# Self attention of a decoder layer: when the scores are made and when their exponentials are issued

## The chip, the cores and the metric

The kernel runs on one core of a Trainium2 chip. The time is device microseconds (us) of one execution; before the change it is 2971.65 us, the median of three runs (2970.52 to 2972.86). The core has one matrix engine (PE, with its weight loads shown apart as PEld), the engines DVE, ACT and POOL, and SP, which issues the DMAs. Matrix results land in PSUM, which this kernel uses as eight banks of 512 fp32 columns on 128 partitions.

## The reference, cut to what matters

A small encoder over 2 x 77 rows gives the memory; then a decoder layer runs over x, which is (2, 2048, 512) in fp32: causal self attention, cross attention, and a feed-forward of width 2048. There are 16 heads of 32 columns. The part that the change touches is the causal self attention:

```
y = y + _mha(yn, yn, ..., sb)                 # yn = _ln(y), sb = relative bias + causal mask
# in _mha, for each of the 16 heads:
scores = einsum('bhqd,bhkd->bhqk', q, k) / sqrt(32) + bias[None]
attn = softmax(scores, axis=-1)
out = einsum('bhqk,bhkd->bhqd', attn, v)
```

## The kernel before

**Units, pieces, visits.** A unit is one tile of 128 query rows (`t`) of one block of 512 rows (`m`, 0 to 3), for one group of four heads (`g`), in one batch entry (`b`). Unit `n` runs over `b`, `m`, `g`, `t` in this order: 128 units, numbered 0 to 127, with sixteen in a block. A unit at row tile `i = 4m + t` needs the `i + 1` key tiles up to its own; `pieces` cuts them into runs of at most four tiles. In block 3 the runs are 4, 4, 3, 2, or 4, 4, 4 and 2, 3 or 4; in block 2 there are three, in block 1 two, in block 0 one.

**Five steps.** I call them S, E, T, V and the slot. S (`scores`, lines 344 to 393) makes one piece of scores for four heads: eight matmuls (line 361) into four banks, one bank for each head; DVE then copies each bank to SBUF and takes its row maximum (line 370), adding the bias for the last two tiles (line 377). When the unit's last piece is there, line 384 reduces the pieces' maxima to one negated maximum, once for each head, right behind that head's last copy. E is the exponential of one head's whole row, in place, on ACT (line 387). T (`turn`, 397 to 418) transposes the probabilities of up to two pieces: in blocks 1 to 3 each load takes one key tile of all four heads into one bank (line 411), and the bank is copied to `pts`, three of eight loads by DVE (line 415) and then five by ACT (line 417). V (`values`, 420 to 440) multiplies by the values into one bank (line 428), and ACT copies that bank out (line 436, or 439 for pieces after the first). The slot (`slot(n + 1)`) issues other work: a projection (lines 206, 217, 230 and 242, eight matmuls of 512 columns), transposes for the softmax's division (line 453) and for the norm (line 294), in some blocks parts of the encoder or of the first cross attention, and all DMA issues, on SP.

**The order is written out by hand.** Every engine runs its instructions in the order in which the program issues them. `bank()` deals the eight banks in turn: an S takes four, a T one for each load, a V one, a projection one. The loop from line 1264 makes a visit for each pair of pieces:

```
turn(pair)                       # T, then one E: exps(1) at line 418
if ends and n + 1 < end:
    slot(n + 1)
if may_score():
    score_next()
while may_score() and (len(pair) > 1 or units[n][1] == 0):
    score_next()
exps(3 if units[n][1] == 1 else 1)
values(pair)                     # V
```

A unit of block 2 or 3 has two visits, called a and b below ("visit 36b"); the slot is in b. `may_score` (line 1246) lets a piece of unit `n` be scored once unit `n - 2` has been transposed that far, because the two share a place in `pp`. E of blocks 1 to 3 waits in the list `late_exps` until `exps(k)` issues the first `k` of it; in block 0 it is issued at once. Ahead of a unit's first T, everything of that unit that still stands in `late_exps` is issued.

**Two orders, written out.** S38(0-3) is the score step of key tiles 0 to 3 of unit 38, E38.0 the exponential of its head 0, T8 a transposition of eight key tiles. Block 2 and block 3 before:

```
36a: T7 E37.0 S38(0-3) E37.1 V7
36b: T2 E37.2 slot S38(4-7) E37.3 V2
37a: T8 S38(8-10) S39(0-3) S39(4-7) E38.0 V8
37b: T2 E38.1 slot S39(8-11) E38.2 V2
38a: E38.3 T8 E39.0 S40(0-3) S40(4-6) E39.1 V8
...
52a: T8 E53.0 S54(0-3) S54(4-7) E53.1 V8
52b: T5 E53.2 slot S54(8-11) S54(12-14) E53.3 V5
53a: T8 E54.0 ...
```

Of the kernel before, what the change touches and what calls it, by code (L numbers as in the profile page):

```python
# [11 lines left out]
AF = mybir.ActivationFunctionType  # L12
ALU = mybir.AluOpType
AX = mybir.AxisListType
# [3 lines left out]
P = 128  # L18
# [4 lines left out]
HC = P // HD  # L23
# [31 lines left out]
def tile_encoder_decoder(ctx: ExitStack, tc: tile.TileContext, ins, out):  # L55
    nc = tc.nc
# [92 lines left out]
    with (  # L149
# [20 lines left out]
        def bank():  # L170

            i = count["bank"] % count["banks"]
            count["bank"] += 1
            return psum[:, i, :]
# [6 lines left out]
        def rows4(r):  # L181
            return slice(r * HD, (r + 1) * HD)


        nTs, qTs, ots, sums_of = {}, {}, {}, {}
# [132 lines left out]
        units = [(b, m, g, t) for b in range(B) for m in range(NMB) for g in range(NC) for t in range(TB)]  # L318
# [13 lines left out]
        def probabilities(n):  # L332
            w = (units[n][1] + 1) * MB
            at = END - HC * w if n % 2 else 0
            return [pp[:, at + r * w : at + (r + 1) * w] for r in range(HC)]

        late_exps = []

        def exps(k):

            for _ in range(min(k, len(late_exps))):
                late_exps.pop(0)[1]()

        def scores(n, k0, kn):
            b, m, g, t = units[n]
            i = m * TB + t
            if k0 == 0:
                state[n] = {
                    "p": probabilities(n),
                    "mx": sm.tile([P, HC, 8], F32, name="mx", tag="mx"),  # L350
                    "nm": sm.tile([P, HC], F32, name="nm", tag="nm"),
                    "col": 0,
                }
                if t == 0:
                    sums_of[b, m, g] = sm.tile([P, TB, HC], F32, name="sums", tag="sums")
            st = state[n]
            last = k0 + kn == i + 1
            q = qTs[b, m, g]
            banks = [bank() for _ in range(HC)]
            for r in range(HC):  # L360
                nc.tensor.matmul(  # L361
                    banks[r][:, : kn * P], q[rows4(r), ts(t, P)], kT[rows4(r), g, k0 * P : (k0 + kn) * P],
                    start=True, stop=True,
                )
            far = max(0, kn - 2) if last else kn
            col = st["col"]
            for r in range(HC):
                p, s, c = st["p"][r], banks[r], col
                if far:
                    nc.vector.tensor_scalar(  # L370
                        p[:, k0 * P : (k0 + far) * P], s[:, : far * P], 1.0, None, ALU.mult, ALU.max,
                        accum_out=st["mx"][:, r, c : c + 1],
                    )
                    c += 1
                if last:
                    w = (kn - far) * P
                    nc.vector.tensor_tensor_reduce(  # L377
                        p[:, (i + 1) * P - w : (i + 1) * P], s[:, far * P : kn * P],
                        biases[b, m, g][:, r, 2 * P - w :], 1.0, LOWEST, ALU.add, ALU.max,
                        accum_out=st["mx"][:, r, c : c + 1],  # L380
                    )
                    c += 1
                    nm = st["nm"][:, r : r + 1]
                    nc.vector.tensor_reduce(nm, st["mx"][:, r, :c], AX.X, ALU.max, negate=True)  # L384

                    def run(p=p[:, : (i + 1) * P], nm=nm, to=sums_of[b, m, g][:, t, r : r + 1]):
                        nc.scalar.activation(p, p, AF.Exp, bias=nm, accum_out=to)  # L387

                    if m:
                        late_exps.append((n, run))  # L390
                    else:
                        run()
            st["col"] = c

        got = {}

        def turn(pieces):

            first = units[pieces[0][0]][1] == 0
            loads = []  # L400
            for n, k0, kn in pieces:
                ks = range(k0, k0 + kn)
                if first:
                    loads += [[(n, k, r) for k in ks] for r in range(HC)]
                else:
                    loads += [[(n, k, r) for r in range(HC)] for k in ks]
            for o, load in enumerate(loads):
                pt = bank()
                pts = in_turn("pts", pts_all).rearrange("p (x q) -> p x q", q=P)
                for x, (n, k, r) in enumerate(load):  # L410
                    nc.tensor.transpose(pt[:, ts(x, P)], state[n]["p"][r][:, ts(k, P)], ident)  # L411
                    got[n, k, r] = pts[:, x, :]
                w = len(load) * P
                if o % 2 if first else o < 3 * len(loads) // 8:
                    nc.vector.tensor_copy(pts[:, : len(load), :], pt[:, :w])  # L415
                else:
                    nc.scalar.copy(pts[:, : len(load), :], pt[:, :w])  # L417
            exps(1)

        def values(pieces):  # L420

            n = pieces[0][0]
            b, m, g, t = units[n]
            ks = [k for _, k0, kn in pieces for k in range(k0, k0 + kn)]
            ot = bank()[:, :P]
            for k in ks:
                for r in range(HC):
                    nc.tensor.matmul(  # L428
                        ot[rows4(r), :], vv[:, k, ts(g * HC + r, HD)], got.pop((n, k, r)),
                        start=(k == ks[0]), stop=(k == ks[-1]),  # L430
                    )
            if t == 0 and ks[0] == 0:
                ots[b, m, g] = in_turn("oT", oT_all)
            dst = ots[b, m, g][:, ts(t, P)]
            if ks[0] == 0:
                nc.scalar.copy(dst, ot)
            else:
                more = sm.tile([P, P], F32, name="more", tag="more", bufs=1)
                nc.scalar.copy(more, ot)  # L439
                nc.gpsimd.tensor_tensor(dst, dst, more, ALU.add)  # L440
# [538 lines left out]
        def slot(n):  # L979
            for f in light[n]:  # L980
                f()
            for _, run, _ in jobs[n]:
                load_next()
                run(loaded[ran[0]])
                ran[0] += 1
            if n == 5:
                load_next()
# [35 lines left out]
        def w_1_load(i):  # L1023

            nc.sync.dma_start(w_1[:, :, ts(i, D)], wchunk("dec_ff1_wT", i * D))
# [220 lines left out]
        def may_score():  # L1246

            if at[0] == len(stream):
                return False
            n, k0, kn = stream[at[0]]  # L1250
            same = n >= 2 and units[n][:2] == units[n - 2][:2]
            return n < 2 or turned_to[n - 2] >= (min(k0 + kn, size[n - 2]) if same else size[n - 2])

        def score_next():
            n, k0, kn = stream[at[0]]
            scores(n, k0, kn)
            scored_to[n] = k0 + kn
            at[0] += 1
# [4 lines left out]
        i = 0  # L1263
        while i < len(stream):
            n = stream[i][0]
            pair = [p for p in stream[i : i + 2] if p[0] == n]
            while scored_to.get(n) != size[n]:
                score_next()
            while any(u == n for u, _ in late_exps):
                exps(1)  # L1270
            ends = pair[-1][1] + pair[-1][2] == size[n]
            if ends:
                for f in ahead[n + 1]:
                    f()
            turn(pair)
            if n == end - 2:
                for _, k0, _ in pair:
                    w_1_load(k0 // 4)
            turned_to[n] = pair[-1][1] + pair[-1][2]
            if ends and n + 1 < end:  # L1280
                slot(n + 1)
            if may_score():
                score_next()
            while may_score() and (len(pair) > 1 or units[n][1] == 0):
                score_next()
            exps(3 if units[n][1] == 1 else 1)
            values(pair)
            i += len(pair)

# [72 lines left out]
```

## Time and profile before

| | |
|---|---|
| median of three runs | 2971.65 us |
| the profiled execution's own time | 2971.24 us |
| its span, first to last instruction | 2969.5 us |
| PE, PEld busy | 2881.6 us, 2061.6 us |
| DVE, ACT, POOL busy | 2013.0 us, 1421.8 us, 763.4 us |
| mean granted clock of PE | 0.990 |
| PE busy, idle from 189 to 1828 us (from the first batch entry's block 1 to the end of self attention) | 1589.0 us of 1639.0, 50 us |
| line 370, DVE, score copy of 512 columns | 687 ns, next one 0.61 us after its start |
| line 377, DVE, score copy with bias, 256 columns | 417 ns |
| line 384, DVE, the four reductions of a unit | 156 ns each, 512 of them |
| line 387, ACT, E of 1408 / 1664 / 1792 / 1920 / 2048 columns | 1471 / 1708 / 1814 / 1911 / 2016 ns |
| line 417, ACT, copy of a transposed bank | 603 ns, next one 0.48 us after its start |

Self attention takes the first 1828 us of the span; its blocks start at about 26, 189, 410 and 650 us, and for the second batch entry at 949, 1089, 1294 and 1533 us. Cross attention of the other blocks and the feed-forward follow.

How to read it: the profile shows one execution. Busy times are the union of an engine's instructions, and the ends of matmuls are modelled, so a PE that is shown busy can still start its next matmul late. The distance from the start of one step on PE to the start of the next, in the timeline, shows that lateness. In a row of the timeline the columns are start, duration, engine, line, operation and operands, and in brackets the idle time of the engine before it with what ended it.

### The profile page before, as it was taken

Reading aid. Unit: us, or ns where it says so; the run is one execution under the profiler, and the core shown is the slowest. Engines: PE = TensorE matmul, PEld = TensorE weight load, DVE = VectorE, ACT = ScalarE, POOL = GpSimd, SP = SyncE. Lnnn points to the kernel's source line nnn. Section 1 sums busy time; section 2 is a strip of 40 time slices with the busy share of each in tenths; the row PEclk is TensorE's granted clock in tenths of the full one; section 3 lists DMA queues with packets and bytes.
Section 4 is the critical chain, followed back from the end, with each engine's and each line's share of the span. In section 5 each row is a group of like instructions: output and inputs, shape, how many; then the busy total and the mean of one; then the engine's idle time right before and its main releaser. Section 6 shows DMA issues by size and latency. Waiting matters only on the chain. (4 is left out here: it accounts for less than half of the span.)

```text
span 2969.5 us, 61184 instructions
## 1 busy us (share of the span) xinstructions
PE 2881.6 (97%) x24440; PEld 2061.6 (69%) x24440; DVE 2013.0 (68%) x5782; ACT 1421.8 (48%) x2767; POOL 763.4 (26%) x658
## 2 busy tenths in 40 slices
PE   8899999999999999999999999999999999999999
PEld 5557666666676556666666776787777687877788
DVE  4766577777876778777767784656565656565645
ACT  3345456656666446566657675223232323232321
POOL 0100000000000101001000004464646374646465
PEclk9899999999999999999999999999999999999999
DMA  6413301201111512201201113200001000000000
GB/s 175 98 49 115 95 15 55 62 16 44 34 41 55 135 26 65 69 26 58 58 15 37 37 34 125 80 29 1 29 1 38 9 29 1 29 1 29 1 15 15
DMA packets 117648, 137.14 MB, mean 46 GB/s; under 512 B 18240, under 2 KB 73072, under 8 KB 117234
## 3 DMA queue, kind: packets, MB, share of 16 engines
q1 hardware_dynamic: 117362, 133.22, 15.4%
q8 instruction: 192, 3.15, 0.4%
q14 instruction: 94, 0.77, 0.1%
HBM read 111.33 MB, written 21.86 MB: 45 GB/s over the span
## 5 line engine op out<-in xcount | busy, mean ns | idle before, releaser
L387 ACT ACTIVATE pp<-pp,nm 128x128 f32<-128x128 f32 (+15 forms) x512 | 615.6, 1214 | 162.8 <-DVE nm L384 160.1
L370 DVE TENSOR_SCALAR_CACHE_REDUCE pp<-psum 128x512 f32<-128x512 f32 (+3 forms) x1024 | 554.4, 590 | 115.4 <-PE psum L361 113.6
L411 PE MATMUL psum<-ident,pp 128*128 128x128 f32 x4352 | 544.5, 278 | 44.1 <-ACT pp L387 32.3
L411 PEld LDWEIGHTS psum<-ident,pp 128*128 128x128 f32 x4352 | 475.9, 142 | 106.5 <-ACT pp L387 39.3
L417 ACT COPY pts<-psum 128x512 f32<-128x512 f32 (+2 forms) x744 | 379.4, 586 | 196.9 <-PE psum L411 157.1
L1120 POOL TENSOR_TENSOR vv<-pp 128x512 f32<-128x512 f32 x320 | 428.2, 1353 | 167.3 <-PE psum L1137 147.5
L361 PE MATMUL psum<-kT,q 32*128 32x512 f32 (+3 forms) x2560 | 355.5, 564 | 2.6 <-ACT kT L222 1.6
L428 PEld LDWEIGHTS psum<-pts,vv 128*32 128x32 f32 x8704 | 228.9, 111 | 122.3 <-DVE pp L370 77.6
L428 PE MATMUL psum<-pts,vv 128*32 128x128 f32 x8704 | 283.6, 278 | 6.9 <-DVE pp L370 4.2
L440 POOL TENSOR_TENSOR oT<-oT,more 128x128 f32<-128x128 f32 x64 | 29.2, 457 | 1003.6 <-ACT more L439 1003.6
L361 PEld LDWEIGHTS psum<-kT,q 32*128 32x128 f32 x2560 | 158.9, 184 | 177.2 <-issue 92.9
L415 DVE COPY pts<-psum 128x512 f32<-128x512 f32 (+2 forms) x392 | 237.2, 649 | 36.8 <-PE psum L411 36.5
L1152 DVE TENSOR_TENSOR kT<-kT,psum 128x512 f32<-128x512 f32 x256 | 166.7, 680 | 114.6 <-PE psum L1137 107.5
L377 DVE CUSTOM_DVE_ANT_0 pp<-psum,bias 128x256 f32<-128x256 f32 (+1 forms) x512 | 209.5, 409 | 23.0 <-PE psum L361 15.7
L1155 ACT ACTIVATE kT<-kT,vecs 128x256 f32<-128x256 f32 x256 | 115.1, 499 | 192.5 <-DVE kT L1152 192.5
L1166 PE MATMUL psum<-vv 128*128 128x256 f32 x768 | 176.9, 381 | 0.0
L1150 ACT COPY kT<-psum 128x512 f32<-128x512 f32 x124 | 69.6, 588 | 205.1 <-DVE kT L1152 135.4
L1137 PE MATMUL psum<-oT,vv 128*128 128x256 f32 x736 | 166.5, 380 | 0.0
L1166 PEld LDWEIGHTS psum<-vv 128*128 128x128 f32 x768 | 143.1, 190 | 26.8 <-issue 9.5
L1137 PEld LDWEIGHTS psum<-oT,vv 128*128 128x128 f32 x736 | 138.8, 190 | 24.3 <-issue 6.2
L1120 DVE TENSOR_TENSOR vv<-kT 128x512 f32<-128x512 f32 x160 | 133.1, 846 | 15.5 <-PE psum L1166 14.5
L276 POOL TENSOR_TENSOR rstd<-rstd,mhalf 128x1 f32<-128x1 f32 x32 | 18.2, 568 | 404.8 <-DVE rstd L275 345.4
(176 smaller groups left out, 4028.4 us busy)
## 6 DMA issues: line engine op xcount, KB each, us to landing
wqk<-in_dec_sa_in_wT_dram SPq DMA_DIRECT2D x64, 256.0 KB, 3.6
bias<-tz SPq DMA_DIRECT2D x128, 128.0 KB, 3.5
wbig<-in_dec_sa_in_wT_dram SPq DMA_DIRECT2D x8, 1024.0 KB, 7.4
vv<-in_enc_ff_wT_dram SPq DMA_DIRECT2D x8, 1024.0 KB, 5.2
wbig<-in_dec_sa_out_wT_dram SPq DMA_DIRECT2D x8, 1024.0 KB, 7.7
vv<-y SPq DMA_DIRECT2D x32, 256.0 KB, 3.3
out_dram<-vv SPq DMA_DIRECT2D x32, 256.0 KB, 2.0
xt<-in_x_dram SPq DMA_DIRECT2D x30, 256.0 KB, 3.9
```

Source lines behind the costliest of these rows:

```text
L361: nc.tensor.matmul(banks[r][:, : kn * P], q[rows4(r), ts(t, P)], kT[rows4(r), g, k0 * P : (k0 + kn) * P], start=True, stop=True,)
L370: nc.vector.tensor_scalar(p[:, k0 * P : (k0 + far) * P], s[:, : far * P], 1.0, None, ALU.mult, ALU.max, accum_out=st["mx"][:, r, c : c + 1],)
L377: nc.vector.tensor_tensor_reduce(p[:, (i + 1) * P - w : (i + 1) * P], s[:, far * P : kn * P], biases[b, m, g][:, r, 2 * P - w :], 1.0, LOW ...
L387: nc.scalar.activation(p, p, AF.Exp, bias=nm, accum_out=to)
L411: nc.tensor.transpose(pt[:, ts(x, P)], state[n]["p"][r][:, ts(k, P)], ident)
L415: nc.vector.tensor_copy(pts[:, : len(load), :], pt[:, :w])
L417: nc.scalar.copy(pts[:, : len(load), :], pt[:, :w])
L428: nc.tensor.matmul(ot[rows4(r), :], vv[:, k, ts(g * HC + r, HD)], got.pop((n, k, r)), start=(k == ks[0]), stop=(k == ks[-1]),)
L1120: engine.tensor_tensor(dst, quarter(*parts[0], n), quarter(*parts[2], n), SIGN[parts[1]])
L1137: nc.tensor.matmul(mm[:, ts(f, TOK)], a[:, c, ts(f, P)], b[:, c, :], start=(c == 0), stop=(c == 1))
L1152: nc.vector.tensor_tensor(dst, dst, got, SIGN[sign])
L1166: nc.tensor.matmul(mm[:, t, :], lhs[:, c, ts(t, P)], rhs[:, c, :], start=(n == 0 and c == 0), stop=(n == 3 and c == 1),)
```

## The change

Two things change. In `scores`, the four reductions of line 384 become one instruction over all four heads, issued behind the last head's copy, and the four E come behind it. In the loop, at most two pieces of scores are issued in a visit, now also in a visit of a single piece (where it was one), and `exps(1)` ahead of V becomes `exps(2)` (it stays 3 in block 1).

```diff
@@ scores
                     c += 1
-                    nm = st["nm"][:, r : r + 1]
-                    nc.vector.tensor_reduce(nm, st["mx"][:, r, :c], AX.X, ALU.max, negate=True)
-
-                    def run(p=p[:, : (i + 1) * P], nm=nm, to=sums_of[b, m, g][:, t, r : r + 1]):
-                        nc.scalar.activation(p, p, AF.Exp, bias=nm, accum_out=to)
-
-                    if m:
-                        late_exps.append((n, run))
-                    else:
-                        run()
             st["col"] = c
+            if not last:
+                return
+
+            nc.vector.tensor_reduce(st["nm"], st["mx"][:, :, :c], AX.X, ALU.max, negate=True)
+            for r in range(HC):
+                p, nm, to = st["p"][r][:, : (i + 1) * P], st["nm"][:, r : r + 1], sums_of[b, m, g][:, t, r : r + 1]
+
+                def run(p=p, nm=nm, to=to):
+                    nc.scalar.activation(p, p, AF.Exp, bias=nm, accum_out=to)
+
+                if m:
+                    late_exps.append((n, run))
+                else:
+                    run()
@@ the loop
-            if may_score():
-                score_next()
-            while may_score() and (len(pair) > 1 or units[n][1] == 0):
-                score_next()
-            exps(3 if units[n][1] == 1 else 1)
+
+            for _ in range(2):
+                if may_score():
+                    score_next()
+            exps(3 if units[n][1] == 1 else 2)
             values(pair)
```

The same visits, in the new order, as the loop's rules give them:

```
36a: T7 E37.2 S38(0-3) E37.3 V7
36b: T2 slot S38(4-7) S38(8-10) E38.0 E38.1 V2
37a: T8 E38.2 S39(0-3) S39(4-7) E38.3 V8
37b: T2 slot S39(8-11) E39.0 E39.1 V2
38a: T8 E39.2 S40(0-3) S40(4-6) E39.3 V8
38b: T3 slot S40(7-8) E40.0 E40.1 V3
39a: T8 E40.2 S41(0-3) S41(4-7) E40.3 V8
39b: T4 slot S41(8-9) E41.0 E41.1 V4
40a: T7 E41.2 S42(0-3) E41.3 V7
...
52a: T8 S53(8-11) S53(12-13) E53.0 E53.1 V8
52b: T5 E53.2 slot S54(0-3) S54(4-7) E53.3 V5
53a: T8 S54(8-11) S54(12-14) E54.0 E54.1 V8
```

## The prediction

> **What bounds the kernel now.** I read the page first, then the waits, then the timeline of a few visits. PE looks full:
>
> ```profile
> PE 2881.6 (97%) x24440; PEld 2061.6 (69%) x24440; DVE 2013.0 (68%) x5782; ACT 1421.8 (48%) x2767; POOL 763.4 (26%) x658
> ```
>
> Its idle time from 189 to 1828 us is 50 us, but a PE shown busy can be late. In the timeline a T8 takes 3.55 us from its start to the next step's when nothing holds it, an S of 512 columns 0.95, a V8 1.88, a projection 3.53. Over these bounds the visits of that stretch lose about 171 us. So PE's own work sets the time, and losses come at few places. In block 2 they are two:
>
> ```profile
> 485.07 4.99 PE L361 MATMUL psum<-kT,q 32*128 32x384 f32 x24
> 499.95 3.39 PE L411 MATMUL psum<-ident,pp 128*128 128x128 f32 x29 [1.42 <-ACT pp L387]
> ```
>
> The first row (visit 37a) is three S in a row: 4.93 us to the next step, 2.6 without a wait; the third S needs the first one's banks back (lost: 2.33). The second (38a) is T8 behind E38.3 (lost: 1.74). The Trainium skill ("Perfetto Trace Analysis", section Identifying the Most-Contended Engine) calls matmul busy time a poor measure of headroom and takes weight-load time instead; by the 97% at most 50 us could be had here, by its 69% hundreds. The starts, with 171, stand between.
>
> What an E does that reaches the head of ACT's queue before its maximum exists is in the trace already, at visits 62b and 63a, where fresh scores of unit 64 get their E at once and E63.3 stands behind them:
>
> ```profile
> 927.40 0.26 ACT L387 ACTIVATION_READ_ACCUMULATOR pp<-pp,nm 128x1 f32 x1
> 928.72 0.40 ACT L387 ACTIVATE pp<-pp,nm 128x128 f32<-128x128 f32 x1 [1.06 <-DVE nm L384]
> ...
> 930.31 1.99 ACT L387 ACTIVATE pp<-pp,nm 128x2048 f32<-128x2048 f32 x1
> 932.20 0.19 ACT L387 ACTIVATION_READ_ACCUMULATOR pp<-pp,nm 128x1 f32 x1
> 932.29 0.24 ACT L439 COPY more<-psum 128x128 f32<-128x128 f32 x1
> ```
> ```profile
> 932.44 4.88 PE L411 MATMUL psum<-ident,pp 128*128 128x128 f32 x29 [2.43 <-ACT pp L387]
> ```
>
> ACT stands 1.06 us for DVE, everything behind waits, V's copy (line 439) comes last, and T8 of 63a loses 4.25 us.
>
> **The change part by part.** *One reduction for four.* DVE's price of a unit's last piece:
>
> ```profile
> 486.02 0.29 DVE L370 TENSOR_SCALAR_CACHE_REDUCE pp<-psum 128x128 f32<-128x128 f32 x1 [0.74 <-PE psum L361]
> 486.23 0.08 DVE L370 DVE_READ_ACCUMULATOR pp<-psum 128x1 f32 x1
> 486.23 0.42 DVE L377 CUSTOM_DVE_ANT_0 pp<-psum,bias 128x256 f32<-128x256 f32 x1
> 486.58 0.08 DVE L377 DVE_READ_ACCUMULATOR2_ANT mx<- 128x1 f32 x1
> 486.69 0.16 DVE L384 TENSOR_REDUCE nm<-mx 128x1 f32<-128x4 f32 x1
> 486.77 0.28 DVE L370 TENSOR_SCALAR_CACHE_REDUCE pp<-psum 128x128 f32<-128x128 f32 x1
> ```
>
> A head takes 0.75 us (486.02 to 486.77), 0.19 of it from the reduction (486.58 to 486.77), so 0.555 without. A head with 256 columns takes 0.345, with 256 + 256 0.69. At the end comes one reduction, taken as 0.28 with its wait (0.11 + 0.16; bounds: 0.16, no wait, and 0.63, four rows). So a unit saves 0.5 us of DVE, 64 us over 128 units, nearly all beside PE; but head 0 can begin only with head 3. The Trainium skill ("VectorE: DVE Perf Modes", The TRN2 errata) says that an instruction pays a fixed latency whatever its size, so fewer is better; read alone it makes this a gain of 3 x 128 x 0.156 = 60 us. The waits show PE's transposes waiting for line 377's work only 9.9 us in all, so I book no more than 0.3 to 0.5 us at the T of block 1.
>
> *The moved S and E.* Two old losses go: in block 2 the third S and the E in front of T8. But before, a unit's last S came about a visit ahead of its first E; now two E follow it at once. On ACT they stand ahead of V's copy, of the next T's five copies and of the next E. And a T8 behind a V needs eight banks: the eighth is V's own. So T8 waits for V's copy, which waits for two E, which wait for DVE.
>
> Visit 36b into 37a, from the start of S38(4-7) on PE (0). DVE begins at 1.15 (479.78 to 480.94 in the timeline), copies four heads at 0.61 (3.6), four at 0.555 (5.8), reduces (6.1). E38.0 and E38.1 take 1.46 each (start to start): 9.05. V's copy ends at 9.35. PE has done S 0.95, S 0.75, V2 0.57 and seven of T8's banks by 5.3; the eighth starts at 9.4, T8 ends at 9.9 instead of 5.8: **4.1 us late**. ACT's T copies, from 9.3 at 0.48 each, free the next S's banks by 11.85, which costs 0.8 more: 4.9. The same sum elsewhere:
> - 37b into 38a: DVE 4.25, two E of 1.565, copy 7.65; T8 ends 8.2 for 5.1, the next S another 0.9: 4.0.
> - 38b into 39a: DVE 2.4, E 1.46, copy 5.6; 1.15, and 0.7 at the S: 1.85.
> - 39b into 40a: T7 does not need V's bank, the S behind it does: 0.9.
>
> Four units pay 11.65 and lose the old 5.2 (2.33, 1.74, 0.6 and small ones): +6.5. This holds for units 36 to 43, +13. Units 32 to 35: E32.3 ahead of T7 4.5, 33a 1.4, 34a and 35a and 36a 5.05, less 3.6 (third S in 30 and 31), 2.33 and small ones: +5. Units 44 to 47 end in the next block's scores: +2.5. A block 2 costs 20.5, **both 41 us**.
>
> Block 3, from the end of T8 in a-visits. Last S at 0; DVE from 1.15; two E; V8's copy; the T copies of visit b on ACT; two E; next T8. Unit 53's: 1.15 + 4 x 0.61 + 4 x 0.345 + 0.28 = 5.3 (with the waits 5.5); 2 x 1.775 = 9.1; copy 9.35; four copies of 0.48 = 11.3; 2 x 1.775 = 14.85; T8 from 15.0 to 18.6. Before, ACT began E53.0 as soon as T8's copies were out (739.60, PE's S at 738.85) and had finished E53.3 2.6 us before T8 began. From T8's end to T8's end:
> - t = 0 (52): 18.6; before 17.8.
> - t = 1 (53): 19.6 by the same sum with 15 tiles; before 18.2 to 19.1.
> - t = 2 (54): the slot takes V8's bank, free at 11.0, while PE is there at 6.9: 11.0 + 3.53 + S 1.9 + V7 1.67 + T8 3.6 = 21.7; before 18.3 to 18.7.
> - t = 3 (55): T8 of visit b waits for V8's copy until 8.35, ends at 8.85; then slot 3.53, S 1.9, V8 1.88, T8 3.6: 19.7; before 18.4 to 19.5.
>
> With the norm's transposes in the slot (L294) it is 0.4 to 1.1 more. Units 60 to 62, and 122 to 126, have little or no projection to hide the chain: 18 to 21 against 14.2 to 16.2, and unit 62, where E64 come in between, 24.6 against 18.9. The five S in a row of visit 48 (and 112) go: 18.6 for 29, a gain of 10.3. Fifteen periods: 304.8 for 282.2 in the first batch entry, 295.4 for 272.2 in the second; **both +46 us**.
>
> Block 1: the one E of the next unit in front of V holds V's copy until 8.25 at t = 2 (DVE 6.8, E 1.05), where the slot wants that bank at 7.0: +1.25, and about 0.5 at t = 1, against 0.3 to 0.5 saved at two T: **+4** over 32 units. Block 0: E come up to 1.3 us later, under slots of 3.5 to 11 us of PE work: 0 (bounds -5 and +5). DMAs, on SP, are issued in the slots, whose order does not change. Nothing of cross attention or feed-forward moves.
>
> *The clock.* A PE that waits this long loses its clock:
>
> ```profile
> 929.00:932.15 3.15, 1.01 (x23) 0.57 (x15) 0.80 (x7) 3.15 (x9) 0.00 (x0) 1.00 0.02 5
> 932.15:935.56 3.41, 3.12 (x15) 3.12 (x16) 2.07 (x3) 0.38 (x3) 0.45 (x1) 0.50 0.00 0
> ```
>
> The column ahead of the last two is the granted clock: after the wait in 63a it is 0.50 for 3.41 us, which costs 1.7 us of PE's work. Visit 48 paid 6.8 us at 0.50; the waits of 1.7 us in block 2 paid nothing. The change makes about 35 waits of 2.8 us or more. Bounds: 0, and 35 x 3.4 = 119. I take 20 us (six in ten are followed by one 3.41 us window, as after most of the waits over 2.3 us here, and some four tenths of that is hidden, since PE then waits for ACT's copies anyway).
>
> **Sum.** 41 + 46 + 4 + 0 + 20 = 111 on the profiled execution's own 2971.2 us (span 2969.5): 3082 us. The median of the runs, 2971.65, lies 0.4 above; I leave that out.
>
> **Rivals.**
> - *The old waits go and no new ones come: faster.* If the two E found their maxima ready, gains would stand alone: in block 2 eight visits of 2.33 and eight of 1.74 (33), six third S of 1.81 (11), the five S (15), the E in front of 48a and 49a and their twins (8), T of block 1 (7): -74, 2897 us. It decides if DVE is done within about 2 us of the last S; the rows above (1.15 + 2.45 before the last piece) say 2.4 to 6.8. For it speaks only that ACT is busy 48%.
> - *Half.* The delays are real, but a late PE gives DVE and ACT time to catch up, so that each visit's wait shortens the next's, and the clock holds: (41 + 46 + 4) / 2 = 45: 3016 us.
> - *The clock goes at every wait, two windows long*: 91 + 119: 3181 us.
> - *Nothing to measure*: gains and losses cancel, 2971 us, as if only DVE's reductions had changed.
>
> **How the numbers follow.** Forecast 0.66, half 0.14, clock 0.06, faster 0.10, same 0.04. Changes within 0.2% (6 us) could not be told from none. Predicted 3082 us; the range reaches from below the half case to the forecast with 80 us of clock: 3000 to 3140. Faster 0.10, same 0.04, slower 0.86.
>
> **What would show it.** Right: "ACT pp L387 <- DVE nm" grows from 94 us (189 to 1828 us) to well over 200; PE's line 411 waits long for ACT's line 436 or 439 (V's copy); three S in a row and the E ahead of 38a are gone; blocks 2 take about 260 us for 240, blocks 3 322 for 299; the granted clock falls below 0.98. Wrong: T8 of 37a near 3.6 us, or E38.0 starting less than 3 us behind S38(4-7).

## The result, and the profile after

The changed kernel takes 3107.02 us (median of 4 runs, 3104.61 to 3110.33) for 2972.26 (4 runs, 2970.52 to 2976.46): a ratio of 1.0452, 95% interval 1.0434 to 1.047. It is 135 us slower; I had predicted 111 (3082 us, range 3000 to 3140). The profiled execution's own time is 3107.94 us, its span 3106.1, the mean granted clock 0.972 for 0.990.

The page of the changed kernel, part 1 (busy time and share of the span) and part 5 (busy time, mean of one, idle time of the engine before it):

```profile
PE 2923.7 (94%) x24440; PEld 2086.8 (67%) x24440; DVE 1953.4 (63%) x5398; ACT 1401.1 (45%) x2767; POOL 766.6 (25%) x658
```
```profile
L392 ACT ACTIVATE pp<-pp,nm 128x128 f32<-128x128 f32 (+15 forms) x512 | 614.3, 1209 | 672.0 <-DVE nm L387 672.0
```

The same instructions are there less 384 reductions, and DVE is 60 us less busy. E (now line 392) costs the same 1.21 us each, but ACT stood 672 us for the maxima where it stood 160.1. In the waits of self attention (189 to 1970 us; total, number, longest):

```profile
ACT pp L392 <- DVE nm L387: 593.7, 112, 11.9
PE psum L415 <- ACT more L443: 39.1, 20, 2.9
PE psum L415 <- ACT pp L392: 20.9, 25, 3.0
PE psum L206 <- ACT oT L440: 16.2, 6, 3.8
PE psum L361 <- ACT oT L440: 12.2, 8, 3.8
```

Lines 440 and 443 are ACT's copies of V's bank, 415 the transposes of T. Over the same work before (189 to 1828 us) the first and the third row were:

```profile
ACT pp L387 <- DVE nm L384: 94.3, 29, 10.7
PE psum L411 <- ACT pp L387: 28.2, 23, 2.4
```

So PE's old wait for E itself has fallen a little. The second row and the last two are the new losses of PE: it waits for V's bank, which is copied behind E.

Visit 36b into 37a, where I had worked the sum out step by step, on PE and on ACT:

```profile
496.50 1.82 PE L361 MATMUL psum<-kT,q 32*128 32x512 f32 x16
499.02 4.10 PE L415 MATMUL psum<-ident,pp 128*128 128x128 f32 x28
505.87 1.04 PE L415 MATMUL psum<-ident,pp 128*128 128x128 f32 x4 [2.74 <-ACT more L443]
```
```profile
502.65 1.47 ACT L392 ACTIVATE pp<-pp,nm 128x1408 f32<-128x1408 f32 x1 [8.04 <-DVE nm L387]
504.03 0.18 ACT L392 ACTIVATION_READ_ACCUMULATOR pp<-pp,nm 128x1 f32 x1
504.12 1.45 ACT L392 ACTIVATE pp<-pp,nm 128x1408 f32<-128x1408 f32 x1
505.48 0.19 ACT L392 ACTIVATION_READ_ACCUMULATOR pp<-pp,nm 128x1 f32 x1
505.57 0.24 ACT L443 COPY more<-psum 128x128 f32<-128x128 f32 x1
```

(x28 and x4 are the transposes into T8's first seven banks and into its eighth.) Seven of T8's eight banks are filled at once, the eighth waits until V's copy has gone, and that stands behind two E. E38.0 starts 6.15 us behind S38(4-7) (predicted 6.1), and T8 is 4.27 us late (predicted 4.1). DVE's rows in front of it:

```profile
501.77 0.28 DVE L370 TENSOR_SCALAR_CACHE_REDUCE pp<-psum 128x128 f32<-128x128 f32 x1
501.99 0.08 DVE L370 DVE_READ_ACCUMULATOR pp<-psum 128x1 f32 x1
501.99 0.42 DVE L377 CUSTOM_DVE_ANT_0 pp<-psum,bias 128x256 f32<-128x256 f32 x1
502.33 0.08 DVE L377 DVE_READ_ACCUMULATOR2_ANT mx<- 128x1 f32 x1
502.45 0.17 DVE L387 TENSOR_REDUCE nm<-mx 128x4 f32<-128x16 f32 x1
```

A head now takes 0.56 us for 0.75, as predicted, but this is the fourth head, and E38.0 waits for it.

Blocks from T to T on PE, in both batch entries, and the time at half clock (of all stretches with a granted clock of 0.50):

| us | block 0 | block 1 | block 2 | block 3 | half clock |
|---|---|---|---|---|---|
| before | 163.1, 140.4 | 220.5, 204.6 | 239.6, 239.6 | 299.3, 294.4 | 63.0 |
| after | 170.7, 142.6 | 216.0, 199.8 | 276.2, 278.8 | 332.7, 320.4 | 175.3 |
| after less before | +9.8 | -9.3 | +75.8 | +59.4 | +112.3 |
| predicted, clock apart | 0 | +4 | +41 | +46 | |

### The profile page after: what moved, and what is told of

The parts are those of the page before. It is cut to its first block, busy times and chain, and to the rows that moved or that the text cites. A ratio compares the mean times of both kernels' runs of the same rounds, so it can differ in the third digit from the quotient of the medians.

```text
span 3106.1 us, 60517 instructions
## 1 busy us (share of the span) xinstructions
PE 2923.7 (94%) x24440; PEld 2086.8 (67%) x24440; DVE 1953.4 (63%) x5398; ACT 1401.1 (45%) x2767; POOL 766.6 (25%) x658
## 5 line engine op out<-in xcount | busy, mean ns | idle before, releaser
L415 PE MATMUL psum<-ident,pp 128*128 128x128 f32 x4352 | 561.3, 282 | 76.1 <-ACT more L443 39.1
L415 PEld LDWEIGHTS psum<-ident,pp 128*128 128x128 f32 x4352 | 484.6, 144 | 146.5 <-ACT more L443 43.9
L1124 POOL TENSOR_TENSOR vv<-pp 128x512 f32<-128x512 f32 x320 | 433.1, 1369 | 169.2 <-PE psum L1141 148.5
L361 PE MATMUL psum<-kT,q 32*128 32x512 f32 (+3 forms) x2560 | 356.5, 584 | 19.7 <-ACT oT L440 14.4
L377 DVE CUSTOM_DVE_ANT_0 pp<-psum,bias 128x256 f32<-128x256 f32 (+1 forms) x512 | 196.1, 411 | 23.5 <-PE psum L361 15.7
L1141 PEld LDWEIGHTS psum<-oT,vv 128*128 128x128 f32 x736 | 138.8, 190 | 24.4 <-issue 6.2
L206 PE MATMUL psum<-nT,wqk 128*128 128x512 f32 x256 | 130.3, 657 | 16.2 <-ACT oT L440 16.2
```

What stands on the lines that cost most here:

```text
L361: nc.tensor.matmul(banks[r][:, : kn * P], q[rows4(r), ts(t, P)], kT[rows4(r), g, k0 * P : (k0 + kn) * P], start=True, stop=True,)
L377: nc.vector.tensor_tensor_reduce(p[:, (i + 1) * P - w : (i + 1) * P], s[:, far * P : kn * P], biases[b, m, g][:, r, 2 * P - w :], 1.0, LOW ...
L1124: engine.tensor_tensor(dst, quarter(*parts[0], n), quarter(*parts[2], n), SIGN[parts[1]])
L1141: nc.tensor.matmul(mm[:, ts(f, TOK)], a[:, c, ts(f, P)], b[:, c, :], start=(c == 0), stop=(c == 1))
```

## The experiments

There are ten more kernels. The times are medians, the ratios are to the kernel before on the same chip, and the blocks are measured as above. Each expectation, written before its run, names a theory W, which was mine, and one or two rivals.

| kernel | us | ratio, 95% | block 0 | block 1 | block 2 | block 3 | half clock |
|---|---|---|---|---|---|---|---|
| e1, merged reduction alone | 2956.87 | 0.9938 (0.9926 to 0.9951) | 170.9, 141.2 | 215.9, 199.6 | 236.9, 237.1 | 295.0, 287.0 | 69.4 |
| e4, new loop alone | 2982.92 | 1.0022 (1.0012 to 1.0031) | 162.9, 140.6 | 215.0, 198.8 | 249.1, 250.5 | 297.7, 296.1 | 66.0 |
| e2, merged, two pieces | 3035.62 | 1.0201 (1.0185 to 1.0217) | 169.2, 141.7 | 211.0, 194.7 | 241.9, 243.0 | 331.4, 334.0 | 123.5 |
| e3, merged, two E | 3087.74 | 1.0384 (1.0369 to 1.0398) | 169.1, 141.9 | 222.4, 206.2 | 247.2, 247.2 | 343.3, 337.9 | 132.4 |
| e9, new loop, two reductions | 3002.30 | 1.0099 (1.0078 to 1.012) | 161.8, 138.4 | 211.6, 195.3 | 256.2, 254.6 | 306.0, 303.6 | 86.4 |
| e5, after, V first | 3195.30 | 1.0746 (1.0728 to 1.0764) | 170.6, 142.1 | 250.3, 226.4 | 282.3, 280.0 | 334.5, 339.1 | 226.4 |
| e6, after, PE kept at work | 3085.06 | 1.0377 (1.0362 to 1.0392) | 170.7, 142.4 | 216.0, 199.8 | 272.2, 272.7 | 323.7, 315.6 | 90.7 |
| e7, e2 with three pieces in block 3 | 2951.02 | 0.9923 (0.9907 to 0.994) | 169.2, 141.5 | 211.0, 194.8 | 241.8, 243.0 | 291.2, 285.8 | 72.3 |
| e8, e1 with two pieces in block 2 | 2945.62 | 0.9905 (0.989 to 0.9919) | 171.9, 141.4 | 215.9, 199.6 | 233.5, 233.5 | 291.2, 287.5 | 66.2 |
| e10, e8 with two reductions in block 0 | 2932.80 | 0.9862 (0.9847 to 0.9876) | 162.0, 138.3 | 217.5, 199.6 | 233.5, 233.5 | 291.4, 287.5 | 65.2 |

### The parts, each alone and in pairs

e1 is the kernel before with the changed `scores`. e4 is the kernel after with the reduction put back behind each head's copy:

```diff
+                    nm = st["nm"][:, r : r + 1]
+                    nc.vector.tensor_reduce(nm, st["mx"][:, r, :c], AX.X, ALU.max, negate=True)
...
-            nc.vector.tensor_reduce(st["nm"], st["mx"][:, :, :c], AX.X, ALU.max, negate=True)
```

e2 and e3 keep the merged reduction and one half each of the change to the loop, e2 the two pieces, e3 the second E:

```diff
# e2, against after
-            exps(3 if units[n][1] == 1 else 2)
+            exps(3 if units[n][1] == 1 else 1)
# e3, against e1
-            exps(3 if units[n][1] == 1 else 1)
+            exps(3 if units[n][1] == 1 else 2)
```

What was expected of each:

> Only the single reduction for four heads, in the old loop. Theory W (the time is lost where an E stands at the head of ACT's queue before its maxima exist, and holds V's copy, the next T's copies and so PE): in the old loop the E come a visit behind the last S, so head 0's later start is covered; block 1 gains the 4 to 5 us per batch entry that the changed kernel shows there. 2960 to 2972 us. Rival M (the merged reduction by itself delays the E and is the cause): 3000 us or more.

> The changed loop with the old four reductions, each behind its own head's last copy. Theory W: the E that waits at ACT's head begins 1.2 to 2.2 us earlier (after one head's copies, not four), so each held T8, slot and chain is shorter by that: in block 2 T8 of 37a is 2.5 to 3 us late where it is 4.3, and the whole is 3020 to 3070 us; block 1 gives back its 4 us. Rival S: 3100 to 3115 us.

> The changed kernel with one E ahead of V, as before, in place of two: the new rule for scores and the single reduction stay. Theory W: by the loop's rules block 2 then has its E a visit behind the scores and no three S in a row, so a block 2 falls to 222 to 230 us (before 240, changed 276 to 279); block 3 still makes its scores in the visit before and keeps the long chain of four E, 310 to 325 us (before 299, changed 333). Sum 2960 to 3000 us. Rival S (making scores later, at most two pieces a visit, is the loss, whatever the E do): 3070 us or more, block 2 above 260.

> The old rule for scores, the single reduction, and two E ahead of V. Theory W: with two E in a visit the list runs empty, so that in block 3 the E of a unit now follow its last S at once, ahead of V of the b-visit; the T8 behind waits for V's bank: DVE 6.2, two E 3.7, copy 0.3, against 6.0 at PE, 4 us a unit, and some of it in block 2. 3060 to 3140 us. Rival S: nothing happens without the later scores, 2955 to 2990 us.

e1 lies below what either theory gave it, e4 too; e3 is where theory W had it, and e2's block 3 and block 2 are as neither said. The parts do not add. The merged reduction alone gains 18 us, the loop alone loses 8 (2974.85 on that chip), the two together lose 135. So the merge changes the time by -18 us in the old order and by +124 in the new one (3107.0 against 2982.9). It is the same instruction in both; what the order changes is whether an E already stands at the head of ACT's queue for its result. In e1, where a unit's E come a visit later, its saving also shortens the third S of 37a, 4.99 us before:

```profile
488.91 4.43 PE L361 MATMUL psum<-kT,q 32*128 32x384 f32 x24
```

In the new order with four reductions (e4), the same place as above:

```profile
484.09 1.47 ACT L387 ACTIVATE pp<-pp,nm 128x1408 f32<-128x1408 f32 x1 [6.37 <-DVE nm L384]
485.46 0.19 ACT L387 ACTIVATION_READ_ACCUMULATOR pp<-pp,nm 128x1 f32 x1
485.56 1.45 ACT L387 ACTIVATE pp<-pp,nm 128x1408 f32<-128x1408 f32 x1
486.92 0.19 ACT L387 ACTIVATION_READ_ACCUMULATOR pp<-pp,nm 128x1 f32 x1
487.01 0.24 ACT L439 COPY more<-psum 128x128 f32<-128x128 f32 x1
```
```profile
482.14 4.66 PE L411 MATMUL psum<-ident,pp 128*128 128x128 f32 x28
487.30 0.66 PE L411 MATMUL psum<-ident,pp 128*128 128x128 f32 x4 [0.50 <-ACT more L439]
```

The order on ACT is the same, V's copy behind two E; but E38.0 starts 1.95 us after T8 (482.14 to 484.09), for 3.63 in the changed kernel (499.02 to 502.65), since DVE goes on with heads 1 to 3 while ACT works. PE's wait is 0.50 us for 2.74.

e2 and e3 say where the loop's halves bite. With one E (e2) block 2 is back at 242, but block 3 stays at 331 to 334: with the last piece of a unit a visit later, its last E is caught in front of the next T. On ACT and PE around T8 of 51a in e2:

```profile
699.55 2.00 ACT L392 ACTIVATE pp<-pp,nm 128x2048 f32<-128x2048 f32 x1 [5.79 <-DVE nm L387]
...
709.53 2.00 ACT L392 ACTIVATE pp<-pp,nm 128x2048 f32<-128x2048 f32 x1
```
```profile
709.19 0.55 PE L415 MATMUL psum<-ident,pp 128*128 128x128 f32 x3
711.68 5.05 PE L415 MATMUL psum<-ident,pp 128*128 128x128 f32 x29 [1.94 <-ACT pp L392]
```

E51.0 begins at 699.55, after a wait for the maxima, and the last of the four ends at 711.53: T8, begun at 709.2 on the first heads, waits for it. With the second E and the old pieces (e3) block 3 is slower still. There it is as theory W had it: in that block (690 to 1010 us of e3) T waits 14 times for V's copy of the visit before, 39.0 us in all, and T8 of 53a takes 7.67 us where it takes 4.57 in the changed kernel. Theory W had e2's block 3 at 310 to 325 and its block 2 at 222 to 230; e7 and e8 take that up.

### How much of the late start costs how much

e9 reduces two heads at a time:

```diff
+                if last and r % 2:
+                    nc.vector.tensor_reduce(
+                        st["nm"][:, r - 1 : r + 1], st["mx"][:, r - 1 : r + 1, :c], AX.X, ALU.max, negate=True
+                    )
...
-            nc.vector.tensor_reduce(st["nm"], st["mx"][:, :, :c], AX.X, ALU.max, negate=True)
```

> The changed kernel with two reductions of two heads each in place of one of four. With one a head (e4) the time was 2982.9, with one for all 3107.0. Theory W (what counts is how late the first E of a unit may start, with ScalarE's four E, 1.2 to 1.5 us each, in a row behind it: one head's copy, two heads' copies, or four, at 0.55 to 0.75 us a copy): a place between, with a third to a half of the 124 us, 3020 to 3050; T8 of 37a between 5.75 and 7.81, and ScalarE's wait for the maxima between those of the two kernels. Rival T (a threshold: waits under some 3 us are covered and cost no clock, so that one head more changes little): 2980 to 3000, half-clock windows near e4's 66 us. Rival N (the number of reductions on VectorE counts, not the start of E): at or under 2983.

3002.3 us, between what the two theories gave. T8 of 37a on PE and the first E on ACT:

```profile
481.47 4.29 PE L418 MATMUL psum<-ident,pp 128*128 128x128 f32 x28
487.19 0.66 PE L418 MATMUL psum<-ident,pp 128*128 128x128 f32 x4 [1.44 <-ACT more L446]
487.78 2.96 PE L361 MATMUL psum<-kT,q 32*128 32x512 f32 x16
```
```profile
483.98 1.47 ACT L395 ACTIVATE pp<-pp,nm 128x1408 f32<-128x1408 f32 x1 [6.92 <-DVE nm L384]
```

E38.0 starts 1.95, 2.51 and 3.63 us after T8's start with four, two and one reduction, and T8 takes 5.75, 6.31 and 7.81: 3.80, 3.80 and 4.18 more. So at this place there is no threshold in the wait itself; T8 follows E's start one for one, and the 0.38 extra in the changed kernel is its last four transposes at half clock (0.97 us to the next S for 0.59). In blocks 2 and 3 together the steps from four to two and from two to one are +27 and +88 us, about 1 to 3, where E's start moves by 0.56 and 1.12, 1 to 2; the time at half clock goes from 66 to 86 to 175 us. Two things show in block 3, from T8's end to T8's end. A small delay is partly covered: unit 53 takes 17.78, 18.12 and 19.25 us with four, two and one reduction. And where half clock follows, it comes on top: unit 54 takes 20.15, 20.85 and 25.13, of the last 2.9 gone when the clock is kept up (22.23 in e6, below). My third to a half of 124 also left out that blocks 0 and 1 gain 10 us with two reductions.

### Whose place in ACT's queue

e5 issues V, and so its copy, ahead of the two E:

```diff
-            exps(3 if units[n][1] == 1 else 2)
             values(pair)
+            exps(3 if units[n][1] == 1 else 2)
```

> The changed kernel with one thing moved: V is issued before the two E of the visit, so that V's copy stands ahead of E in ScalarE's queue; E's own start does not depend on V (V ends about 0.6 us after S, the maxima come 3 us after it). Theory W (ScalarE's chain E, E, copies of T sets the end, whichever bank is the first to be missed): T8 of visit 37a gets its eighth bank and no longer waits, but the two S after it wait for the banks whose copies stand behind the two E; only V's copy (0.24 us) leaves the chain, so a visit gains a few tenths and block 2 falls by less than 12 us in 277; the idle time is moved, not removed: 3070 to 3105, the low end if the shorter single waits also spare half-clock windows. Rival B (V's bank is the cause: what TensorE waits for by name, 70 us under the tile of V's copy in the whole table of waits, goes): 3040 or less, T8 and the S after it both at their undisturbed times.

3195.3 us: both theories fell. In block 2 what theory W said of the stall is there: T8 of 37a is only 0.92 us late, but the two S behind it are 2.28 and 2.46 late and V, at half clock, 1.69. On PE and ACT:

```profile
530.73 4.54 PE L415 MATMUL psum<-ident,pp 128*128 128x128 f32 x32
535.19 2.10 PE L361 MATMUL psum<-kT,q 32*128 32x512 f32 x6
537.89 4.02 PE L361 MATMUL psum<-kT,q 32*128 32x512 f32 x10 [0.60 <-ACT pts L421]
541.84 3.64 PE L432 MATMUL psum<-pts,vv 128*32 128x128 f32 x64
```
```profile
530.87 0.27 ACT L443 COPY more<-psum 128x128 f32<-128x128 f32 x1 [4.57 <-PE psum L432]
534.35 1.47 ACT L392 ACTIVATE pp<-pp,nm 128x1408 f32<-128x1408 f32 x1 [3.22 <-DVE nm L387]
```

What W missed is the other visits: there V's copy, now in front, makes ACT stand for PE while maxima lie ready. Into visit 27a, in block 1 (the reduction of unit 27's maxima began at 361.99):

```profile
379.64 0.27 ACT L440 COPY oT<-psum 128x128 f32<-128x128 f32 x1 [11.78 <-PE psum L432]
379.80 1.15 ACT L392 ACTIVATE pp<-pp,nm 128x1024 f32<-128x1024 f32 x1
380.86 0.19 ACT L392 ACTIVATION_READ_ACCUMULATOR pp<-pp,nm 128x1 f32 x1
380.95 1.14 ACT L392 ACTIVATE pp<-pp,nm 128x1024 f32<-128x1024 f32 x1
```

ACT stood 11.78 us, then ran two E of the unit whose T8 PE had just reached; that T8 was 4.06 us late. Block 1 alone lost 61 of the 88 us (250.3 and 226.4 for 216.0 and 199.8). The queue's head blocks whatever stands there: an E too early holds V's copy, a V's copy too early holds E.

### The price of the clock

e6 is the kernel after with transposes that are already done issued again, in T8's seventh load, while PE would otherwise stand for the eighth bank:

```diff
                     nc.tensor.transpose(pt[:, ts(x, P)], state[n]["p"][r][:, ts(k, P)], ident)
+                u, row = units[load[0][0]], units[load[0][0]][3]
+                more = 0
+                if o == 6 and u[1] == 2 and sum(p[2] for p in pieces) == 8:
+                    more = {1: 7, 2: 5}.get(row, 0)
+                if o == 6 and u[1] == 3 and pieces[0][1] == 8 and row == 2:
+                    more = 8
+                for _ in range(more):
+                    for x, (n, k, r) in enumerate(load):
+                        nc.tensor.transpose(pt[:, ts(x, P)], state[n]["p"][r][:, ts(k, P)], ident)
```

> The changed kernel with the transposes of T8's seventh load issued again (7 or 5 times over in visits a of t=1 and t=2 of block 2, 8 times in visit b of t=2 of block 3; same bank, same result), so that TensorE works through the stretch in which it otherwise stands; nothing that ScalarE or VectorE waits for comes earlier. It measures the price of the clock by itself. Theory W (part of the loss is the half clock that follows a long stand: 33 windows, 175.3 us in the changed kernel's trace against 12, 63.0 us before): the waits of S and E stay, the windows of half clock fall below 100 us in all, and the time falls by 20 to 45 us, to 3060 to 3090. Rival (the windows lie where TensorE would wait anyway, so the clock costs nothing of its own): 3100 to 3115, also if the windows go. Above 3120: the added transposes lie on the path, and the run says nothing.

3085.1 us, as theory W had it: 22 less with 640 matmuls more on PE. Visit 50b, T7 and the projection behind it, in stretches (length, then busy time of PE, PEld, DVE, ACT and POOL with their instructions, the granted clock, and DMA); first the changed kernel, then e6:

```profile
735.60:742.70 7.10, 3.30 (x33) 3.05 (x29) 3.90 (x19) 4.33 (x6) 0.00 (x0) 0.92 0.01 2
742.70:749.10 6.40, 6.40 (x10) 2.48 (x10) 0.00 (x0) 6.31 (x9) 0.00 (x0) 0.56 0.00 0
```
```profile
731.10:738.20 7.10, 6.81 (x64) 6.53 (x60) 3.96 (x19) 4.27 (x6) 0.00 (x0) 1.00 0.01 2
738.20:741.80 3.60, 3.58 (x8) 1.44 (x8) 0.00 (x0) 3.60 (x6) 0.00 (x0) 1.00 0.00 0
```

T7 takes 7.1 us in both, so the wait is the same; but the projection takes 6.4 us at a clock of 0.56 after a stand, 3.6 at 1.00 after work. Over the kernel, half clock falls from 175.3 to 90.7 us (84.6) and the profiled span by 23.5, so 0.28 us for each.

That rate is too low, because at two places, T8 of 33a and its twin 97a, the repeated transposes lie on the path. There T8 had hardly waited; its end in the changed kernel, and in e6 the repeated transposes in front of its last bank:

```profile
435.86 3.74 PE L415 MATMUL psum<-ident,pp 128*128 128x128 f32 x29 [0.47 <-ACT pp L392]
```
```profile
436.91 3.22 PE L425 MATMUL psum<-ident,pp 128*128 128x128 f32 x28
```

T8 of 33a takes 7.75 us for 4.69, and from its start to the end of V the two visits are 2.5 and 2.7 us longer. Without these 5.2 us e6 saves 28.7, 0.34 for each us of half clock. By the two rates the change's whole 112.3 us more of half clock cost an estimated 31 to 38 of its 135 us.

### The order in blocks 2, 3 and 0

e8 keeps before's loop and its one E, but takes at most two pieces in a visit of block 2, also in a visit of a single piece, and at most three elsewhere, so that the five S of visit 48 go too; e7 takes at most three in block 3 and two in the others, in single pieces' visits as well; e10 is e8 with e9's two reductions for `m == 0` only:

```diff
# e8, in place of "for _ in range(2)", exps(1) as before
+            for _ in range(2 if units[n][1] == 2 else 3 if len(pair) > 1 or units[n][1] == 0 else 1):
# e7
+            for _ in range(3 if units[n][1] == 3 else 2):
# e10
+                if last and m == 0 and r % 2:
...
+            if m:
                 nc.vector.tensor_reduce(st["nm"], st["mx"][:, :, :c], AX.X, ALU.max, negate=True)
```

> Before's loop with the merged reduction and before's single E in the step, and the limit of two pieces in a visit for block 2 alone, single pieces' visits there too; in blocks 1 and 3 before's rule with at most three pieces. Theory W (the merged reduction is a gain wherever a unit's E are taken a visit or more after its last piece, and two pieces in a visit end the wait of the third S, 1.8 us at 33a, 37a, 41a, 45a, if E does not follow the maxima at once): below e1's 2956.9, namely 2940 to 2954, block 2 at 228 to 235 for 237, block 3 at 287 to 296 as in e1. Rival (the second piece in the visits of single pieces makes E late again as in e2, where T8 of t=1 lost 0.9 and its S 1.0): 2955 to 2970, block 2 at 238 or more.

> e2 with up to three pieces in a visit in block 3, two elsewhere, single pieces' visits too; it differs from e8 in the entry into block 2: at most two pieces in visits 30 and 31, so that the last piece of unit 32 and its E come in visit 31 and E32.3 stands ahead of T7 of 32a. Theory W (that entry is why e2's block 2 took 242 us and not the 222 to 230 that I expected: T7 of 32a +5.3, T8 of 33a and 34a +1.6 each, less two third S of 1.8 in block 1; and e2's block 3, at 331 us for 287 to 295 in e1, came from the limit of two in block 3): 2946 to 2958, above e8's 2945.6, block 2 at 240 to 245, block 3 at 288 to 300. Rival 1 (the second piece in single pieces' visits makes block 3 slow): 2990 or more, block 3 at 315 or more. Rival 2 (the entry is worth nothing): within 3 us of e8.

> e8 with two reductions of two heads each in block 0, where E are issued at once, and one reduction elsewhere. Theory W (the late start of E is also what the merged reduction costs in block 0, which the forecast set at nothing: 169 to 172 us in the first batch entry and 141 to 143 in the second in every kernel with one reduction, 162 and 138 with two, 163 and 140 with four): 2931 to 2940, block 0 at 160 to 164 and 137 to 140, blocks 1, 2 and 3 as in e8. Rival (block 0's 8 us follow from something else that those kernels share, such as where their code or their buffers lie): 2943 to 2948, block 0 at 169 or more.

All three came out as theory W had it (2945.6, 2951.0 and 2932.8 us), but for e7's block 3 in the second batch entry, 2 us lower, and e10's first block 1, 1.6 us above e8's. e7's block 3 at 291 and 286 shows that the two-piece limit there made e2's 331 and 334. Its block 2 takes 8 to 10 us more than e8's, of it 5.1 at T7 of 32a (8.29 us for 3.20 in e8), while its block 1 takes 5 less; so the entry from block to block matters, and two pieces in block 2 are a gain where one E follows. e10 is faster than both kernels of this study, 40 us faster than the one before (ratio 0.9862).

e10 also settles block 0, where E are issued at once. Line 556 or 561 is a step of the encoder in the slot, which needs V's bank next; in e8 and in e10:

```profile
94.48 1.32 PE L556 MATMUL psum<-pp 32*77 32x77 f32 x26 [2.53 <-ACT oT L440]
95.73 6.30 PE L206 MATMUL psum<-nT,wqk 128*128 128x512 f32 x8
```
```profile
91.36 0.77 PE L561 MATMUL psum<-pp 32*77 32x77 f32 x26 [1.32 <-ACT oT L445]
92.06 5.40 PE L206 MATMUL psum<-nT,wqk 128*128 128x512 f32 x8
```

The same chain as in block 2: maxima, four E, V's copy, and PE waits 2.53 us with one reduction, 1.32 with two. Over the first block 0 PE's waits for V's copy (line 440 or 445) come to 11.7 us in e8 and to 5.1 in e10.

## Why the prediction was right, and where its sizes were off

**Sign and mechanism: right.** PE is held by V's copy behind E behind DVE; the rows of 37a show it, e4 and e9 move it by moving E's start, and ACT's wait grew as said. The old losses went as said (no S of three pieces, the five S of visit 48: 8.4 us from T8 to V8 for 19.2). Of the rivals, "the old waits go and no new ones come", "half" and "nothing to measure" are out, and "the clock at every wait" too: it wanted 119 us of clock, and e6's rates give 31 to 38.

**The sum: 111 against 135.** The total is nearer than its parts, for they partly cancel: by blocks, after less before is off by +10 in block 0, -13 in block 1, +35 in block 2 and +13 in block 3, against the 20 that I had booked apart for the clock.

**Block 2: +41 was too small.** The steady visits fit: T8 of 37a 4.27 late for 4.1 and the next S 0.92 for 0.8, 38a 3.25 and 0.97 for 4.0 in all, 39a 1.80 for 1.85. Four units cost 8.2 and 9.9 us for the 6.5 booked, and with the clock restored (e6) 7.4 and 7.2. The edges were off: units 32 to 35 took 11.4 and 10.9 us more in the changed kernel where I had 8.6 (5, and the 3.6 that belong to block 1), with T7 of 32a and of its twin 6.3 and 5.3 us late (5.0 and 5.2 in e6) for my 4.5; units 44 to 47 took 6.9 and 8.5 more (5.6 in e6) for 2.5. Of the 75.8 us some 15 are clock, by e6 without its 5.2 us on the path; the other 60 stand against the 41, and the 7.2 that belong to block 1.

**Block 3: +46 against +59.4.** In e6, where fewer stands are followed by half clock, it is +24.4 and +21.2 = 45.6. So the sum of waits fits, and the rest is clock. It fits by units too: from T8's end to T8's end units 52 to 55 take 18.0, 19.3, 22.2 and 20.1 us in e6, for 18.6, 19.6, 21.7 and 19.7.

**Clock: 20 against an estimated 31 to 38.** The term had a right kind and a small size: my "some four tenths hidden" fits roughly (0.28 to 0.34 us of 0.5 possible for each us at half clock, so three to four tenths are hidden), but the windows were more, 112 us in place of 21 x 3.4 = 71.

**Block 1: +4 against -9.3.** Most of it is bookkeeping: visits 30, 31 and their twins, without the third S, took 8.4 us less; 7.2 of this I had booked under block 2. The rest is -0.9 where I had +4. The terms that I named are there: behind T of t = 2 the slot begins later (unit 18: 4.75 us from T's start; 4.18 before, 3.62 in e1), so by 1.13 for my 1.25, and T of t = 1 is 0.56 shorter (unit 17: 2.82 us for 3.38) for my 0.3 to 0.5. Added up over the eight groups of four units the terms as I gave them make 6 us or more, not 4; as measured they make about 4. What I did not have are gains that outweigh them, such as at the first T of each block 1 (2.24 us for 3.18 and 3.19). What the merge gains here alone (4.6 and 5.0 in e1) does not carry over: with the new loop and four reductions (e4) block 1 is 1 us shorter in each batch entry than in the changed kernel.

The rule of the Trainium skill that I had weighed for the merge ("VectorE: DVE Perf Modes", The TRN2 errata: a fixed latency for each instruction, so fewer are better) would have made the merge a gain of 60 us; it gains 18 where E come later (e1) and loses 124 where they do not, so the rule prices DVE and not who waits for it.

**Block 0: 0 against +9.8.** The step that E there lie "under slots of 3.5 to 11 us of PE work" failed: the slot itself begins with work that needs V's bank, as e8 and e10 show. The bound of +5 was too low.

**What no step had** is how the parts hang together. I took the new loop for the cause and the merge for a small thing that starts E later; even with e1's and e4's expectations I put the loop without the merge at 3020 or more, and it is 2983. The late start of head 0, which the prediction names in half a sentence and counts in its sums but does not price apart, is most of the loss: 124 of 135 us by e4.

**Open:** how e9's step from two reductions to one divides between waits and half clock over all of blocks 2 and 3 was read at a few units only (53 and 54 above). Why block 1's other visits gain what they do was not traced.

## What to carry to other kernels

Before merging small instructions, ask who takes the first of their results: where the consumer comes much later the merge is a gain, where it stands at the head of its queue every producer behind the first is added to the wait, and to all that stands behind it in that queue. Price an in-order queue by its head: what is issued there early and not ready holds copies that free banks, and in e5 turning the two round only swapped who waits. Idle time of the waiting engine does not give the price: ACT stood 473 us in e4 for 94 before (189 us to the end of self attention), at a cost of 8 us.

## What the runs showed of the hardware

The clock's loss is a cost of its own: after stands of 2.74 us (37a) and 3.80 us (50b) PE ran some 3.4 and 6.4 us at 0.53 and 0.56, after 0.50 (e4) it did not slow. Work that computes nothing new, put into the stand, kept it at 1.00 and made the kernel 22 us faster, though at 33a and 97a it lay on the path, with PE's busy time 38 us higher (2961.4 for 2923.7) and 2.6% more matmuls: neither busy time nor instruction count of PE told what the kernel would take.
